# Two edits to a sparse-attention and expert layer: the compressed branch multiplied with the exponentials stationary, and 24 instead of 64 sums of ranks

## The chip, the cores and the metric

The kernel runs on one core of a Trainium2 chip. The metric is the device time of one execution in microseconds (us). Five engines work side by side, each through its own queue in order: TensorE (PE in the profile, its weight loads PEld), VectorE (DVE), ScalarE (ACT), GpSimd (POOL) and SyncE (SP), which here issues the DMAs.

## The reference

The input is x of 8 sequences, 512 tokens, 256 channels. It is normalised, and two branches are added to it.

```python
xn = _layernorm(x)
x + _L0_attn_ref(xn, ...) + _L0_ffn_ref(xn, ...)
```

Attention has 16 heads of 16 channels. Keys and values are compressed in blocks of 16 tokens (32 blocks). Every token attends in three ways, and gates add the three outputs:

```python
s_b = einsum('bhtd,bhnd->bhtn', q, k_c) / scale
logits_c = where(c_ok, s_b, NEG)                    # 32 compressed blocks
out_c = einsum('bhtn,bhnd->bhtd', softmax(logits_c), v_c)
_, top_idx = top_k(logits_c, 4)                     # four blocks chosen: out_s over their tokens
out = gates[..., 0:1]*merge(out_c) + gates[..., 1:2]*merge(out_s) + gates[..., 2:3]*merge(out_l)
return out @ Wo
```

The second branch is a gated layer of 1024 hidden units plus a product-key expert layer: four heads, each with two sets of 64 keys. The eight best of each set give 64 sums, and the eight best of these choose the experts.

```python
sc, ix = top_k(sim, 8)                              # sx, sy: eight each, in falling order
all_sc = (sx[..., :, None] + sy[..., None, :]).reshape(b, t, H, 64)
scores, pk = top_k(all_sc, 8)
w = silu(einsum('btd,bthkd->bthk', hidden_states, de)) * softmax(scores)
experts_states = einsum('bthk,bthkd->btd', w, ue)
```

## The kernel before

Each sequence (a "row") is cut into four tiles of 128 tokens, so there are 32 tiles t, with t.i = 0 to 3 the place in the row. All stages are Python generators, one job each, that go through the rows, the tiles or the halves of a row (two tiles): layernorm, prepare_keys, prepare_values, queries, logits, select, compressed, weights, products, finish(0), finish(1), choose_experts, route, experts, hidden, project and some small ones.

The order of the instructions is planned when the program is built, by the class Conductor. A job yields the engine that it wants next and the buffers or events that it needs; the Conductor starts the job that can begin first, and among those within 0.12 us of it the one of lowest rank (the tile number plus a constant of the stage; compressed has +0.3). What each instruction will take is booked from a small table: a matmul of fp32 as 1.68 ns for each moving column divided by the number of strips that run side by side (con.share), a DVE instruction as 0.07 us and 1.04 ns an element, and so on. It also books that DVE and POOL instructions with two SBUF inputs keep each other waiting. The engines then run in the order that came out, whatever the real times are.

Buffers come from a Stock: taking one waits until it is free in the plan. The names that matter here:

- banks: four single PSUM banks of 512 fp32 columns; pairs: two double ones for logits and weights. All other PSUM work shares the four. products holds two of them as accumulators until finish has copied them.
- acss: two SBUF buffers for copies of PSUM, used by compressed and by both finish jobs.
- atcs, attnTs: two each. atc is the compressed branch's output by token; attnT is the transposed sum of the three branches, freed when project has multiplied it with Wo.
- vc17s: per row, the compressed values of all heads, 17 columns a head (16 and a one for the sum), block-diagonal over four heads: partitions are 4 heads by 32 blocks.

The compressed branch of a tile (compressed, line 827): exponentials of the 16 x 32 logits on ACT, four transposes into a bank, copy to ecT (4 heads x 32 blocks on the partitions, 128 tokens in the columns, four groups g). Then 16 products, of 32 columns of vc17 as the stationary operand with the 128 tokens of ecT moving, four at a time in the four column strips of the array; the result has channels on the partitions. ACT copies it to an acs; the branch then waits for an atc and an attnT; by_token (line 809) transposes the copy back in four pieces, and DVE divides by the sum and multiplies with the gate. by_token serves the two finish jobs as well. The heads in atc stand in the order j, g (head 4g + j); finish adds its half of them on POOL.

In choose_experts (line 974) DVE finds the eight best and their places of eight sets (top, ixu), makes two comparison tables (big, at_x), then the 64 sums (sums, 8 x 8 for each of four heads), and for each head MAX8 (best) and MATCH_REPLACE8, which marks the eight best in pick. A threshold turns the marks into 0 and 1; the sum over j counts for each i how many partners are chosen (cnt). at_x is multiplied with it, et becomes the exponentials of the ranks, and later sums is filled with their products, multiplied with pick and summed to row. route then builds the 1024 gate weights with DVE and three POOL multiplications or additions of 1024 elements for each of four heads (big, gw).

All engine calls go through one helper at line 160, so the profile shows L160 for every instruction; they are told apart by the names of their tiles (cst holds the identity: psum<-cst,acs is the transposition of an acs).

Of the kernel before, what the change touches and what calls it, by code (L numbers as in the profile page):

```python
# [12 lines left out]
ALU = mybir.AluOpType  # L13
# [3 lines left out]
P = 128  # L17
# [13 lines left out]
NX = NEXP // NK  # L31
EPS = 1e-5
D1 = D + 1

OUT = -1.0e30
BIG = 3.0e38
# [218 lines left out]
def tile_kernel(ctx, tc, x, wq, wk, wqT, wv, wo, wck, wcv, wga, bga, wgu, bg, bu, wd, bd,  # L255
# [98 lines left out]


    v17s, vl17s = stock("v17_", 2, [P, NT, H * D1 + D]), stock("vl17_", 2, [P, NT - 1, 8 * D1 + D])
    vc17s = stock("vc17_", 2, [P, H * D1 + D])
    for st_, fill in ((v17s, 1.0), (vl17s, 0.0), (vc17s, 0.0)):
        for it in st_.items:
            pool.memset(it[0], fill)  # L360
# [40 lines left out]
    top, ixu = buf("top", [P, 2 * PH, KPH]), buf("ixu", [P, 2 * PH, KPH], U32)  # L401
    ix = buf("ix", [P, KPH, 2 * PH], BF16)
    at_x = buf("at_x", [P, KPH, NX, PH], BF16)
    sums, pick = buf("sums", [P, PH, KPH, KPH]), buf("pick", [P, PH, KPH, KPH])
    best, row = buf("best", [P, PH, KPH]), buf("row", [P, PH, KPH])
    cnt, et = buf("cnt", [P, KPH, PH], BF16), buf("et", [P, 2 * PH, KPH])
    past, rz = buf("past", [P, PH, KPH]), buf("rz", [P, PH])
# [401 lines left out]
    def by_token(acs, dst, gates):  # L809

        pt = yield PE, banks
        p4 = pt.ap.rearrange("p (a g d) -> p a g d", a=4, g=4)
        for a in range(4):
            pe.transpose(p4[:, a].rearrange("p g d -> p (g d)"), acs.ap[:, a, :], ident)
        acs.free()
        rzn = yield DVE, rzs
        po = p4.rearrange("p a g d -> p (a g) d")
        vec.reciprocal(rzn.ap, po[:, :, D])
        n = gates.shape[1]
        for b in range(n):  # L820
            c = slice(16 // n * b, 16 // n * (b + 1))
            vec.scalar_tensor_tensor(dst[:, c], po[:, c, :D], gates[:, b:b + 1],
                                     bc(rzn.ap[:, c], 2, D), ALU.mult, ALU.mult)
        pt.free()
        rzn.free()

    def compressed(t):

        s, i = t.row, t.i
        yield ACT, t.ev("ec")  # L830
        act.activation(t.ec.ap, t.ec.ap, AF.Exp)
        pt, ecT = yield PE, banks, ecTs
        for g in range(4):
            pe.transpose(heads4(pt.ap)[:, g, :],
                         t.ec.ap[:, 4 * g:4 * g + 4, :].rearrange("p h n -> p (h n)"), ident)
        t.ec.free()
        yield ACT,
        act.copy(ecT.ap, heads4(pt.ap))
        pt.free()
        yield None, s.ev("vc"), s.ev("gates")  # L840

        pt, acs = yield PE, banks, acss
        con.share = 4
        for j in range(4):
            for g in range(4):
                c = D1 * (4 * g + j)
                mm(heads4(pt.ap)[32 * g:32 * g + 32, j, :], s.vc17.ap[:, c:c + 32], ecT.ap[:, g, :],
                   start=j == 0, stop=j == 3, skip_group_check=True, tile_position=(0, 32 * g))
        con.share = 1
        ecT.free()  # L850
        t.done("pc")
        yield ACT,
        act.copy(acs.ap, heads4(pt.ap))
        pt.free()
        t.atc, t.attnT = yield None, atcs, attnTs
        yield from by_token(acs, t.atc.ap, s.gt.ap[:, 2, i:i + 1])
        t.done("atc")

    def weights(t):
# [85 lines left out]
    def finish(jp):  # L945
        def body(t):
            s, i = t.row, t.i
            yield None, t.ev("pv"), t.ev("atc")
            acs, at2h = yield ACT, acss, at2s
            act.copy(acs.ap, heads4(t.acc[jp].ap))  # L950
            t.acc[jp].free()
            at2 = at2h.ap
            yield from by_token(acs, at2.rearrange("p b j (g d) -> p (b j g) d", d=D),
                                s.gt.ap[:, 0:2, i])
            t.done(f"at{jp}")
            at = at2[:, 0].rearrange("p j d -> p (j d)")
            yield POOL,
            pool.tensor_tensor(at, at, at2[:, 1].rearrange("p j d -> p (j d)"), ALU.add)
            pool.tensor_tensor(at, at, t.atc.ap[:, 8 * jp:8 * jp + 8, :].rearrange("p h d -> p (h d)"),
                               ALU.add)  # L960
            t.done(f"sum{jp}")
            pt = yield PE, banks
            pe.transpose(pt.ap[:, :P], at, ident)
            at2h.free()
            yield ACT,
            act.copy(t.attnT.ap[:, jp, :], pt.ap[:, :P])
            pt.free()
            t.done(f"attn{jp}")
            if jp == 1:
                yield None, t.ev("sum0")  # L970
                t.atc.free()
        return body

    def choose_experts(t):

        i = t.i
        yield None, t.row.ev("xn")
        pt = yield PE, banks
        for kc in range(2):
            mm(pt.ap, t.row.xnT.ap[:, kc, i * P:(i + 1) * P], wf_s[:, kc, :], start=kc == 0,  # L980
               stop=kc == 1)
        sim = pt.ap.rearrange("p (h k) -> p h k", k=NK)
        for h in range(2 * PH):
            if h % 2 == 0:
                yield DVE,
            vec.max(out=top[:, h, :], in_=sim[:, h, :])
            vec.max_index(out=ixu[:, h, :], in_max=top[:, h, :], in_values=sim[:, h, :])

        t.ed = yield DVE, eds
        ed = t.ed.ap  # L990
        vec.tensor_tensor(ed[:, :, :NK], sim[:, PH:, :], bc(top[:, PH:, 0], 2, NK), ALU.subtract)
        vec.tensor_tensor(ed[:, :, NK:], sim[:, :PH, :NX], bc(top[:, :PH, 0], 2, NX), ALU.subtract)
        pt.free()
        vec.tensor_copy(ix.rearrange("p j h -> p h j"), ixu)

        ayh = yield DVE, bigs
        at_y = ayh.ap.bitcast(BF16).rearrange("p (j y h) -> p j y h", y=NK, j=KPH)
        vec.tensor_tensor(at_y, bc(ytab, 1, KPH), bc(ix[:, :, PH:], 2, NK), ALU.is_equal)
        yield DVE,
        vec.tensor_tensor(at_x, bc(ytab[:, :NX], 1, KPH), bc(ix[:, :, :PH], 2, NX), ALU.is_equal)  # L1000

        vec.tensor_tensor(sums, bc(top[:, :PH, :], 3, KPH), bc(top[:, PH:, :], 2, KPH), ALU.add)
        for h in range(PH):
            if h % 2 == 0:
                yield DVE,
            flat = sums[:, h].rearrange("p i j -> p (i j)")
            vec.max(out=best[:, h, :], in_=flat)
            vec.match_replace(out=pick[:, h].rearrange("p i j -> p (i j)"),
                              in_to_replace=best[:, h, :], in_values=flat, imm_value=BIG)
        yield DVE,  # L1010
        vec.tensor_scalar(pick, pick, HALF_BIG, None, ALU.is_gt)
        with nc.allow_low_precision(reason="counts up to 8"):
            vec.tensor_reduce(cnt.rearrange("p j h -> p h j"), pick, AX.X, ALU.add)


        vec.tensor_tensor(at_x, at_x, bc(cnt, 2, NX), ALU.mult)
        vec.tensor_tensor(et, top, bc(top[:, :, 0], 2, KPH), ALU.subtract)
        yield ACT,
        act.activation(et, et, AF.Exp)
        act.activation(ed, ed, AF.Exp)  # L1020
        pt, t.rc = yield PE, banks, rcs
        pr = pt.ap[:, :PH * (NK + NX)]
        for j in range(KPH):
            rank = bconst("ranks")[:, j * P:(j + 1) * P]
            mm(pr[:, :PH * NK], rank, at_y[:, j].rearrange("p y h -> p (y h)"),
               start=j == 0, stop=False, skip_group_check=True)
        for j in range(KPH):
            mm(pr[:, PH * NK:], identb, at_x[:, j].rearrange("p x h -> p (x h)"),
               start=False, stop=j == KPH - 1, skip_group_check=True)
        ayh.free()  # L1030
        yield ACT,
        for lo, n in ((0, NK), (PH * NK, NX)):
            act.copy(t.rc.ap[:, lo:lo + PH * n].rearrange("p (h y) -> p h y", y=n),
                     pr[:, lo:lo + PH * n].rearrange("p (y h) -> p h y", y=n))
        pt.free()
        yield DVE,
        vec.tensor_tensor(sums, bc(et[:, :PH, :], 3, KPH), bc(et[:, PH:, :], 2, KPH), ALU.mult)
        vec.tensor_tensor(pick, pick, sums, ALU.mult)
        yield DVE,
        vec.tensor_reduce(row, pick, AX.X, ALU.add)  # L1040
        vec.tensor_reduce(rz, row, AX.X, ALU.add)
        vec.reciprocal(rz, rz)
        vec.tensor_tensor(ed[:, :, NK:], ed[:, :, NK:], bc(rz, 2, NX), ALU.mult)

        t.last = yield DVE, lasts
        vec.scalar_tensor_tensor(past, ix[:, :, :PH].rearrange("p j h -> p h j"), float(NX), row, ALU.is_ge, ALU.mult)
        vec.tensor_tensor(past, past, bc(rz, 2, KPH), ALU.mult)
        vec.tensor_reduce(t.last.ap, past, AX.XY, ALU.add)
        t.done("r")
# [199 lines left out]
```

## Time and profile before

| | |
|---|---|
| median of 4 runs | 1877.21 us (1869.95 to 1881.16) |
| profiled execution, its own time | 1877.63 us |
| its span, first to last instruction | 1875.8 us |
| granted TensorE clock | 0.966 |
| PSUM to acs copies on ACT | 96, 55.6 us busy |
| transposes of acs on PE | 384, 55.7 us busy |
| products of ecT with vc17 on PE | 1024 instructions, 34.5 us busy |
| DVE on sums, both uses | 64, 41.7 us busy |
| MAX8 and MATCH_REPLACE8 of the sums | 128 each, 28.1 and 26.7 us busy |

Busy time is the union of the instructions' spans. Matmuls overlap, so that of PE is not the sum of what each costs; the distance from one start to the next in the timeline is nearer to it. A row of the profile reads: line, engine, operation, tiles (output, then inputs), shape, count, then busy us, mean ns of one, and the idle time in front with what ended it. In the timeline a row has the start, the duration, the engine, the operation and the number of instructions merged in it.

### The profile page before, as it was taken

To read this page: it belongs to the slowest core of one execution; us is meant where nothing else is said; L and a number is where in the kernel's file an instruction comes from. 1 tells how busy PE (TensorE), PEld (TensorE's weight loads), DVE (VectorE), ACT (ScalarE), POOL (GpSimd) and SP (SyncE) were. 2 spreads that over 40 slices of the span, in tenths; PEclk is the share of its full clock that TensorE was granted. 3 is DMA by queue.
4 is the path that set the end of the run, shared out by engine and by line. 5 is a ranking of instruction groups with operands and counts; after the bars stand their busy time and mean duration, and the time that the engine had idled before them with its cause. 6 is when DMAs were issued, how large, how long until landed. Compare 5 with 4: busy or idle time off the path is not lost.

```text
span 1875.8 us, 47619 instructions
## 1 busy us (share of the span) xinstructions
PE 1704.3 (91%) x19208; PEld 1277.4 (68%) x19208; DVE 1476.5 (79%) x5292; ACT 692.6 (37%) x1370; POOL 1022.6 (55%) x789
## 2 busy tenths in 40 slices
PE   4899989999989988899899998989989899998989
PEld 2677756777767766677577766767767677676657
DVE  2588897978879789768879868778787877969982
ACT  1343423434245232443334433344333333343133
POOL 2066637545666356655356552756546556474663
PEclk9899989999999999999899999999999999998999
DMA  5010100111000100010000110001000010100000
GB/s 174 10 39 28 31 18 8 35 41 32 24 24 25 36 19 30 24 42 25 15 28 29 36 31 19 18 25 41 25 24 24 19 36 25 30 19 18 29 24 18
DMA packets 55068, 56.11 MB, mean 30 GB/s; under 512 B 21696, under 2 KB 38080, under 8 KB 54848
## 3 DMA queue, kind: packets, MB, share of 16 engines
q1 hardware_dynamic: 54848, 53.07, 9.6%
q8 instruction: 151, 2.47, 0.5%
q14 instruction: 69, 0.57, 0.1%
HBM read 48.02 MB, written 4.19 MB: 28 GB/s over the span
## 4 chain that ended last, share of the span: by engine, by line
PE 62%; DVE 30%; issue 3%; ACT 2%; POOL 1%; SPq 1%; DMA 1%; DVEq 0%; ACTq 0%
PE psum L160 62%; DVE bm L160 4%; DVE big L160 3%; DVE ixu L160 2%; DVE mr L160 2%; DVE pick L160 2%; DVE ml L160 1%; DVE aT L160 1%; DVE at_x L160 1%; DVE sums L160 1%; ACT wT L160 1%; DVE top L160 1%; DVE junk L160 1%; DVE hT L160 1%; DVE xg L160 1%
## 5 line engine op out<-in xcount | busy, mean ns | idle before, releaser
L160 POOL TENSOR_TENSOR big<-big,ed 128x1024 f32<-128x1024 f32 x224 | 488.6, 2181 | 427.8 <-DVE big L160 388.1
L160 ACT ACTIVATE wT<-psum 128x1024 f32<-128x1024 f32 x224 | 219.3, 1023 | 169.5 <-PE psum L160 169.3
L160 PE MATMUL psum<-xnT,wb 128*128 128x256 f32 x1024 | 255.7, 394 | 22.5 <-DVE aT L160 13.7
L160 DVE TENSOR_REDUCE bm<-psum 128x32 f32<-128x512 f32 (+2 forms) x224 | 200.2, 911 | 74.8 <-PE psum L160 74.6
L160 PEld LDWEIGHTS psum<-xnT,wb 128*128 128x128 f32 x1024 | 193.0, 196 | 59.5 <-DVE aT L160 14.5
L160 POOL TENSOR_TENSOR gw<-gw,big 128x1024 f32<-128x1024 f32 x96 | 229.6, 2392 | 6.7
L160 PE MATMUL psum<-k,q 32*128 32x384 f32 (+3 forms) x1024 | 186.6, 469 | 1.6 <-DVE ml L160 1.6
L160 DVE SCALAR_TENSOR_TENSOR big<-rc 128x1024 f32<-128x1024 f32 x128 | 166.2, 1299 | 6.3 <-POOL gw L160 4.0
L160 PE MATMUL psum<-qx,k 32*128 32x128 f32 (+1 forms) x4352 | 154.7, 273 | 11.8 <-DVE ml L160 9.8
L160 PEld LDWEIGHTS psum<-qx,k 32*128 32x128 f32 (+1 forms) x4352 | 128.0, 177 | 49.1 <-issue 30.2
L160 PE MATMUL psum<-wT,v 128*32 128x128 f32 x3584 | 138.2, 279 | 16.1 <-ACT wT L160 15.3
L160 PEld LDWEIGHTS psum<-wT,v 128*32 128x32 f32 x3584 | 87.0, 109 | 80.1 <-ACT wT L160 37.0
L160 PE MATMUL psum<-xnT,deT_s 128*128 128x128 f32 x1024 | 133.2, 285 | 4.1 <-DVE yo L160 1.7
L160 PEld LDWEIGHTS psum<-xnT,deT_s 128*128 128x128 f32 x1024 | 126.3, 200 | 14.1 <-DVE yo L160 1.8
L160 PE MATMUL psum<-wd_s,hT 128*128 128x256 f32 x512 | 125.1, 390 | 3.5 <-DVE hT L160 2.9
L160 DVE SCALAR_TENSOR_TENSOR aT<-aT,psum 128x512 f32<-128x512 f32 x128 | 87.1, 680 | 48.2 <-ACT aT L160 32.7
L160 ACT ACTIVATE xg<-psum,bgh 128x256 f32<-128x256 f32 x128 | 61.0, 477 | 165.1 <-PE psum L160 163.3
L160 PE MATMUL psum<-ue_s,aT 128*128 128x256 f32 x512 | 119.5, 384 | 1.8 <-DVE aT L160 1.8
L160 PEld LDWEIGHTS psum<-wd_s,hT 128*128 128x128 f32 x512 | 95.5, 194 | 21.3 <-DVE hT L160 3.8
L160 PEld LDWEIGHTS psum<-ue_s,aT 128*128 128x128 f32 x512 | 94.6, 190 | 18.4 <-DVE aT L160 2.0
L160 PEld LDWEIGHTS psum<-k,q 32*128 32x128 f32 x1024 | 77.1, 187 | 42.9 <-issue 32.6
L160 DVE SCALAR_TENSOR_TENSOR xg<-psum,xg 128x256 f32<-128x256 f32 x128 | 53.5, 418 | 63.0 <-ACT psum L160 62.8
(161 smaller groups left out, 3193.4 us busy)
## 6 DMA issues: line engine op xcount, KB each, us to landing
wb<-in_wgu SPq DMA_DIRECT2D x128, 256.0 KB, 2.6
xl<-in_x SPq DMA_DIRECT2D x8, 512.0 KB, 4.0
yo<-in_x SPq DMA_DIRECT2D x32, 128.0 KB, 2.1
out<-yo SPq DMA_DIRECT2D x32, 128.0 KB, 1.7
vl<-v SPq DMA_DIRECT2D x96, 8.5 KB, 1.8
deT_s<-in_deT SPq DMA_DIRECT2D x1, 1024.0 KB, 5.2
wd_s<-in_wd SPq DMA_DIRECT2D x1, 1024.0 KB, 7.4
ue_s<-in_ue SPq DMA_DIRECT2D x1, 1024.0 KB, 9.9
```

Of the source, the lines that this page charges most:

```text
L160: return f(*a, **k)
```

## The change

The compressed branch takes each of the four groups of ecT as the stationary operand (128 columns, the tokens) and the 68 columns of vc17 of the four heads of this group as the moving one. The result lies by token at once, heads in order 0 to 15, in one bank. The copy to acs, the transposes and by_token fall away here; DVE divides and scales straight from this bank, and the bank is kept while the branch waits for an atc and an attnT. by_token is left to finish, which now picks its heads from atc through a strided view.

Of the 64 sums of two ranks i and j, only those with (i + 1)(j + 1) at most 8, or a few more, can be among the eight best. Three rectangles hold 24 of them: i = 0 with j = 0 to 7, i = 1 to 3 with j = 0 to 3, i = 4 to 7 with j = 0. sums and pick shrink to 24 columns a head; each filling of sums, the counting into cnt and the summing into row become three instructions, one for a rectangle (for the last, of width 1, a copy in place of a reduction).

```diff
+STEPS = [(0, 1, 8, 0), (1, 3, 4, 8), (4, 4, 1, 20)]
+NS = 24
...
-    vc17s = stock("vc17_", 2, [P, H * D1 + D])
+    vc17s = stock("vc17_", 2, [P, H * D1])
...
-    sums, pick = buf("sums", [P, PH, KPH, KPH]), buf("pick", [P, PH, KPH, KPH])
+    sums, pick = buf("sums", [P, PH, NS]), buf("pick", [P, PH, NS])
...
@@ compressed
-        pt, acs = yield PE, banks, acss
-        con.share = 4
-        for j in range(4):
-            for g in range(4):
-                c = D1 * (4 * g + j)
-                mm(heads4(pt.ap)[32 * g:32 * g + 32, j, :], s.vc17.ap[:, c:c + 32], ecT.ap[:, g, :],
-                   start=j == 0, stop=j == 3, skip_group_check=True, tile_position=(0, 32 * g))
-        con.share = 1
+        pt = yield PE, banks
+        w = 4 * D1
+        for g in range(4):
+            mm(pt.ap[:, g * w:g * w + w], ecT.ap[:, g, :], s.vc17.ap[:, g * w:g * w + w],
+               start=g == 0, stop=g == 3, skip_group_check=True)
         ecT.free()
         t.done("pc")
-        yield ACT,
-        act.copy(acs.ap, heads4(pt.ap))
+        t.atc, t.attnT = yield None, atcs, attnTs
+        rzn = yield DVE, rzs
+        po = by_head(pt.ap[:, :H * D1])
+        vec.reciprocal(rzn.ap, po[:, :, D])
+        vec.scalar_tensor_tensor(t.atc.ap, po[:, :, :D], s.gt.ap[:, 2, i:i + 1], bc(rzn.ap, 2, D),
+                                 ALU.mult, ALU.mult)
         pt.free()
-        t.atc, t.attnT = yield None, atcs, attnTs
-        yield from by_token(acs, t.atc.ap, s.gt.ap[:, 2, i:i + 1])
+        rzn.free()
         t.done("atc")
@@ finish
-            pool.tensor_tensor(at, at, t.atc.ap[:, 8 * jp:8 * jp + 8, :].rearrange("p h d -> p (h d)"),
-                               ALU.add)
+            atj = at.rearrange("p (j g d) -> p j g d", j=2, g=4)
+            pool.tensor_tensor(atj, atj, t.atc.ap.rearrange(
+                "p (g j) d -> p j g d", j=4)[:, 2 * jp:2 * jp + 2], ALU.add)
@@ choose_experts
-        vec.tensor_tensor(sums, bc(top[:, :PH, :], 3, KPH), bc(top[:, PH:, :], 2, KPH), ALU.add)
+        def steps(table):
+            return [table[:, :, o:o + n * w].rearrange("p h (i j) -> p h i j", j=w)
+                    for _, n, w, o in STEPS]
+        def pairs_of(tab):
+            return [(bc(tab[:, :PH, f:f + n], 3, w), bc(tab[:, PH:, :w], 2, n))
+                    for f, n, w, _ in STEPS]
+        for dst, (a, b) in zip(steps(sums), pairs_of(top)):
+            vec.tensor_tensor(dst, a, b, ALU.add)
         for h in range(PH):
...
+            vec.max(out=best[:, h, :], in_=sums[:, h, :])
+            vec.match_replace(out=pick[:, h, :], in_to_replace=best[:, h, :], in_values=sums[:, h, :],
+                              imm_value=BIG)
...
-            vec.tensor_reduce(cnt.rearrange("p j h -> p h j"), pick, AX.X, ALU.add)
+            for (f, n, w, _), p_ in zip(STEPS, steps(pick)):
+                dst = cnt[:, f:f + n, :].rearrange("p j h -> p h j")
+                if w > 1:
+                    vec.tensor_reduce(dst, p_, AX.X, ALU.add)
+                else:
+                    vec.tensor_copy(dst, p_[:, :, :, 0])
...
-        vec.tensor_tensor(sums, bc(et[:, :PH, :], 3, KPH), bc(et[:, PH:, :], 2, KPH), ALU.mult)
+        for dst, (a, b) in zip(steps(sums), pairs_of(et)):
+            vec.tensor_tensor(dst, a, b, ALU.mult)
         vec.tensor_tensor(pick, pick, sums, ALU.mult)
...
-        vec.tensor_reduce(row, pick, AX.X, ALU.add)
+        for (f, n, w, _), p_ in zip(STEPS, steps(pick)):
+            if w > 1:
+                vec.tensor_reduce(row[:, :, f:f + n], p_, AX.X, ALU.add)
+            else:
+                vec.tensor_copy(row[:, :, f:f + n], p_[:, :, :, 0])
```

More of the change, by code (lines that the diff above doesn't have):

```diff
@@ L818, in by_token @@
         vec.reciprocal(rzn.ap, po[:, :, D])
-        n = gates.shape[1]
-        for b in range(n):
-            c = slice(16 // n * b, 16 // n * (b + 1))
+        for b in range(2):
+            c = slice(8 * b, 8 * b + 8)
             vec.scalar_tensor_tensor(dst[:, c], po[:, c, :D], gates[:, b:b + 1],
@@ L1005, in choose_experts @@
                 yield DVE,
[L1006 to L1009, printed above, removed]
+            vec.max(out=best[:, h, :], in_=sums[:, h, :])
+            vec.match_replace(out=pick[:, h, :], in_to_replace=best[:, h, :], in_values=sums[:, h, :],
+                              imm_value=BIG)
         yield DVE,
```

## The prediction

> **What bounds the kernel.** I read the page first, then the chain, then the groups of the two places that are edited, then the timeline around them. The page:
>
> ```profile
> span 1875.8 us, 47619 instructions
> PE 1704.3 (91%) x19208; PEld 1277.4 (68%) x19208; DVE 1476.5 (79%) x5292; ACT 692.6 (37%) x1370; POOL 1022.6 (55%) x789
> PE 62%; DVE 30%; issue 3%; ACT 2%; POOL 1%; SPq 1%; DMA 1%; DVEq 0%; ACTq 0%
> ```
>
> TensorE is the bound and VectorE the second: the chain that ended last lies 62% on one and 30% on the other, and ScalarE and GpSimd hardly appear. So 62% of 1875.8 = 1163 us of PE's 1704 busy us are on the path, 0.68 of it. The chain's own list by line gives DVE pick 1.8% and DVE sums 1.2%, together 56 us; the groups that write these two tiles (11.8 + 26.7 + 12.2 + 21.2 and 26.3 + 15.4) are busy 114 us. So half of this VectorE work is on the path. I use 0.68 and 0.5 as prices of a microsecond of PE and of DVE.
>
> The compressed branch, by groups (count, then busy us, mean ns):
>
> ```profile
> L160 PE MATMUL psum<-cst,acs 128*128 128x128 f32 x384 | 55.7, 280 | 3.7 <-ACT acs L160 3.1 <-DVE atc L160 0.3
> L160 PE MATMUL psum<-ecT,vc 128*32 128x128 f32 x1024 | 34.5, 275 | 2.4 <-ACT ecT L160 2.0 <-ACT qx L160 0.4
> L160 DVE TENSOR_TENSOR sums<-top 128x256 f32<-128x256 f32 x32 | 26.3, 821 | 0.0
> L160 DVE TENSOR_TENSOR et<-top 128x64 f32<-128x64 f32 x32 | 10.8, 337 | 0.0
> ```
>
> An fp32 product is two instructions, a transpose one: 32 a tile for the 16 products, 4 for the transposes (384 over 32 tiles and three uses).
>
> **TensorE.** What one costs is read from distances in the timeline, not from its 0.27 us:
>
> ```profile
> 911.82 0.33 PE L160 MATMUL psum<-cst,at 128*128 128x128 f32 x1 [0.68 <-POOL at L160]
> 912.07 1.08 PE L160 MATMUL psum<-ecT,vc 128*32 128x128 f32 x32
> 913.09 0.33 PE L160 MATMUL psum<-cst,at 128*128 128x128 f32 x1
> ...
> 913.25 1.95 PE L160 MATMUL psum<-xnT,deT_s 128*128 128x128 f32 x16
> ...
> 9.89 1.87 PE L160 MATMUL psum<-wga_s,big 128*128 128x3 f32 x8 [9.89 <-DMA big<-in_wqT]
> ...
> 19.77 2.47 PE L160 MATMUL psum<-hT 128*128 128x128 f32 x10 [0.58 <-DMA hT<-in_keysT]
> ```
>
> Old products: (1.08 - 0.27) / 31 = 0.026 us each, 0.84 a tile, since four column strips run together. New: 4 products, 8 instructions, each with a full 128-column stationary and 68 moving columns. With 128 moving columns one costs (1.95 - 0.28) / 15 = 0.112. Do 68 cost less? The start-up stretch says no: with 3 moving columns the spacing is (1.87 - 0.35) / 7 = 0.22, with 128 it is (2.47 - 0.42) / 9 = 0.23 (PE work runs at half pace there: four transposes take 1.09 at 35.90, later 0.66); loading the stationary sets it. So I take 8 x 0.112 = 0.90, +0.06 a tile, +1.9 us; the other end, pace by columns (0.060 each), would be 0.48, -11.5 us. The code books 4 x 68 columns at 1.68 ns = 0.46 for it, which I do not believe.
> Transposes removed: 4 x 0.11 (eight take 1.04 at 907.83) = 0.44, 14.1 us. Change of array shape: the batch starts 0.25 after the lone transpose and releases the array 0.21 after its own last start, where like follows like in 0.11; two changes of 0.10 go where both neighbours are full-array, none or some are added where a neighbour is tiled. I take one a tile, 3.2 us (0 to 6.4). PE no longer waits for the ScalarE copy: PEld waited 13.2 us for acs in all, a third is 4.4. Sum: -14.1 - 3.2 - 4.4 + 1.9 = -19.8 us of PE; on the path x 0.68 = -13.5.
>
> **ScalarE and GpSimd.** 32 copies of acs at 0.59 go, 19 us of an engine at 37%: hidden by PE, nothing beyond the wait already counted. GpSimd adds atc from a strided view: 64 additions at 0.54; a tenth more is 3 us, hidden (POOL 1% of the chain). The smaller vc17 saves start-up fill only. The DVE division and scaling keep their sizes; since they now wait on a product booked 0.44 us too short, at most 32 x 0.44 = 14 us of DVE waiting, a sixth of it if it hits as rarely as the reciprocals do now (16 waits in 96): about 1 us on the path, left out. Behind a waiting reciprocal on VectorE stand the next evacuations, as now.
>
> **VectorE, work.** Per tile, TENSOR_TENSOR takes 0.42 for 256 and 0.22 for 64 elements, so 0.15 + 1.04 ns each; and a following independent instruction starts 0.08 before the end of the last:
>
> ```profile
> 907.58 0.43 DVE L160 TENSOR_TENSOR at_x<-at_x,cnt 128x512 bf16<-128x512 bf16 x1
> 907.92 0.22 DVE L160 TENSOR_TENSOR et<-top 128x64 f32<-128x64 f32 x1
> 908.06 1.22 DVE L160 TENSOR_REDUCE bm<-psum 128x64 f32<-128x1024 f32 x1
> ```
>
> Each table in three pieces of 32, 48 and 16: 0.185 + 0.20 + 0.17 - 0.16 = 0.39 against 0.42, twice. Each counting or row reduction in three (reductions 0.42 for 256, 0.19 for 32): 0.40 against 0.42, twice. So the splits give 0.10. MAX8 over 24 takes 0.168 (the t<-lg row of that width) against 0.219, four times: 0.20. MATCH_REPLACE8 lies between 0.164 (20 wide) and 0.173 (28) against 0.209, four times: 0.16. pick times sums 0.42 to 0.25: 0.17; threshold 0.29 to 0.21: 0.08. In all 0.71 a tile, 22.7 us.
> [...]
>
> **VectorE, waits for GpSimd.** Two-input instructions stretch when GpSimd works:
>
> ```profile
> 1005.68 1.37 DVE L160 TENSOR_TENSOR at_x<-cbf,ix 128x512 bf16<-128x512 bf16 x1
> 1006.98 2.12 DVE L160 TENSOR_TENSOR sums<-top 128x256 f32<-128x256 f32 x1
> ...
> 1004.33 4.49 POOL L160 TENSOR_TENSOR big<-big,ed 128x1024 f32<-128x1024 f32 x2 [2.71 <-DVE big L160]
> ```
>
> at_x ends when the first POOL product does, sums when the second does: one DVE instruction per POOL instruction, and behind it in VectorE's queue stand the MAX8s and the bm and aT evacuations whose banks PE waits for. The change adds four such instructions and two copies a tile. Each may lose as little as past (mean 0.212 against 0.193 at best, 0.02) or as much as sums<-top (0.82 against 0.42, 0.40). The nearest row is et<-top, small and directly behind another: 0.337 - 0.218 = 0.12. So 6 x 32 x 0.12 = 23 us (4 to 77), which eats the 22.7. I put VectorE at 0 (on the path -9 to +27).
>
> **Banks.** The product's bank is now kept while the branch waits for an attnT; before, an SBUF copy waited. In the seventh tile the batch runs at 391.77, and the attnT it needs comes free at the projection at 404.87; the batches at 613, 1073, 1299 and 1526 wait 14, 3, 17 and 13 us likewise: 60 us with three single banks for four. Against it every tile asks for one bank fewer. PE is busy 28.00 of 28 us in 391 to 419. I take 0; a quarter of PE's pace lost in all 60 us is 15.
>
> **Sum.** The profiled run took 1877.63 us (span 1875.8), 0.4 above the median 1877.21. 1877.6 - 13.5 + 0 + 0 = 1864.1; against the median 1864.
>
> **Rivals.**
> A, the sum: PE falls by 20 us, VectorE stays. 1864, chance 0.45.
> B, slower: the small VectorE instructions meet GpSimd one by one as sums did at 1006.98. At 0.40 each they cost 192 x 0.40 = 77 where the lesser work saves 23: VectorE loses 54, 27 of it on the path, 1877.6 - 13.5 + 27 = 1891. The sign turns where their waits eat both gains: PE's 13.5 and VectorE's 22.7 x 0.5 = 11.4 on the path are 49.8 us of VectorE, over 192 instructions 0.26 each. For it: GpSimd is busy 55%. Against: after at_x, et lost 0.12 only. Chance 0.20.
> C, no change: the bank kept for attnT costs its 15: 1879, or half of that, 1872. Against: one transposing bank less. Chance 0.18.
> D, more: the 68 columns set the pace (another -11.5 - 1.9 = -13, 0.68 of it 9), and small VectorE work is not delayed (-9): 1846. Against: the 3-column row. Chance 0.17.
> The order on every engine is planned anew from the booked costs, so waits move that no row prices; I leave 10 us for that at both ends.
>
> **Numbers.** About 0.5% (9 us) is what a measurement of this kernel can tell from no change. A and D are faster: 0.62; C: 0.18; B: 0.20. The range reaches from D less a part of the re-planning, 1842, to B, 1890.
>
> **What would show it.** Right: no acs use by the branch (64 copies, 256 transposes), ecT as stationary in 256 instructions spaced near 0.11 (0.06 would be D); MAX8 near 0.17; sums pieces whose mean exceeds their best by about 0.12 (0.4 would be B). Wrong: PE waits for atc well above today's 22 us (C), or PE busy falling by 20 us with its idle time growing as much.

## The result: no faster in the order that was drawn

The changed kernel takes 1880.27 us (median of 52 runs) against 1877.96 (78 runs of the kernel before): a ratio of 1.0014 with a 95% interval of 1.0007 to 1.0021. The forecast of 1864 was 16 us too low: the change was to be faster and is not, though 1880 lies inside the range of 1842 to 1890. The page of the changed kernel (span, busy time by engine, share of the chain by engine):

```profile
span 1876.7 us, 46039 instructions
PE 1689.6 (90%) x18312; PEld 1266.1 (67%) x18312; DVE 1486.1 (79%) x5548; ACT 671.1 (36%) x1338; POOL 1012.1 (54%) x789
PE 57%; DVE 34%; issue 3%; ACT 3%; POOL 1%; SPq 1%; DMA 1%; DVEq 0%; ACTq 0%
```

TensorE is busy 14.7 us less (1704.3 before) and the span is 0.9 us longer, so the time in which PE is not busy grew by 15.6 us, from 171.5 to 187.1. VectorE is busy 9.6 us more, though it was given less to do. The groups of the two edited places (count, then busy us, mean ns of one):

```profile
L164 PE MATMUL psum<-vc,ecT 128*128 128x68 f32 x256 | 35.3, 282 | 1.6 <-ACT ecT L164 1.2 <-DVE aT L164 0.4
L164 PE MATMUL psum<-cst,acs 128*128 128x128 f32 x256 | 36.1, 284 | 1.9 <-ACT acs L164 1.7
L164 DVE TENSOR_TENSOR sums<-top 128x32 f32<-128x32 f32 (+2 forms) x96 | 31.9, 385 | 0.0
L164 DVE COPY row<-pick 128x16 f32<-128x16 f32 x32 | 16.4, 511 | 0.0
L164 DVE MAX8 best<-sums 128x8 f32<-128x24 f32 x128 | 22.8, 178 | 0.8
```

The work is what the prediction described: a third of the transposes of acs is gone, 256 products stand in place of 1024, MAX8 takes 0.178 us instead of 0.219. What the products cost is read from the timeline:

```profile
969.11 1.11 PE L164 MATMUL psum<-vc,ecT 128*128 128x68 f32 x8
970.06 0.60 PE L164 MATMUL psum<-cst,gw 128*128 128x128 f32 x4
```

(1.11 - 0.28) / 7 = 0.119 us from one product instruction to the next, and 0.95 from the first to the transposes that follow.

A part of the lost time is seen in PE's waits. PE's waits for atc (in all, times, longest) in the changed kernel, and then the same list before with three neighbours that are used below:

```profile
PE psum L164 <- DVE atc L164: 29.4, 7, 8.0
```

```profile
PE psum L160 <- DVE aT L160: 24.2, 12, 5.9
PE psum L160 <- DVE atc L160: 22.2, 10, 6.2
PE psum L160 <- DVE hT L160: 15.9, 13, 3.0
...
PE psum L160 <- DVE xn L160: 10.1, 7, 6.1
```

Fewer waits for atc, but longer ones. Counting every wait of PE above 2.5 us after the first 40 us of the trace, there are 14 that last 61.0 us together, against 9 with 37.3 us before. One of them, from the timeline of PE in the changed kernel:

```profile
1363.75 0.60 PE L164 MATMUL psum<-cbf 128*128 128x512 bf16 x2
1370.98 2.07 PE L164 MATMUL psum<-kcbd,q 128*128 128x128 f32 x8 [6.62 <-DVE atc L164]
...
1376.20 1.08 PE L164 MATMUL psum<-cst,ext 128*128 128x128 f32 x4 [2.73 <-DVE aT L164]
1377.09 3.66 PE L164 MATMUL psum<-xnT,deT_s 128*128 128x128 f32 x16
```

And the stretches around it (us, then busy time of PE, PEld, DVE, ACT and POOL, then the granted clock, DMA share and GB/s):

```profile
1364.40:1371.00 6.60, 0.02 (x1) 0.03 (x1) 6.43 (x28) 0.00 (x0) 1.53 (x2) 0.77 0.00 0
1371.00:1381.70 10.70, 7.97 (x63) 6.94 (x64) 9.82 (x29) 1.88 (x4) 5.42 (x6) 0.50 0.01 2
1381.70:1395.00 13.30, 12.61 (x170) 9.73 (x169) 12.50 (x25) 5.84 (x12) 7.54 (x3) 1.00 0.15 56
```

PE waits 6.6 us for a bank that VectorE has yet to read; VectorE is busy for 6.43 of these 6.60 us with work that stands before it in its queue. Then the granted clock is 0.50 for 10.7 us: the 16 deT products take 3.66 us, where they took 1.95 in the kernel before, and four transposes 1.08 instead of 0.60. So this long wait is paid a second time, with some 4 us by an estimate (half of the 7.97 busy).

### The profile page after: what moved, and what is told of

Read it like the earlier page. It is cut to its first block, busy times and chain, and to the rows that moved or that the text cites. A ratio compares the mean times of both kernels' runs of the same rounds, so it can differ in the third digit from the quotient of the medians.

```text
span 1876.7 us, 46039 instructions
## 1 busy us (share of the span) xinstructions
PE 1689.6 (90%) x18312; PEld 1266.1 (67%) x18312; DVE 1486.1 (79%) x5548; ACT 671.1 (36%) x1338; POOL 1012.1 (54%) x789
## 4 chain that ended last, share of the span: by engine, by line
PE 57%; DVE 34%; issue 3%; ACT 3%; POOL 1%; SPq 1%; DMA 1%; DVEq 0%; ACTq 0%
PE psum L164 57%; DVE bm L164 5%; DVE big L164 4%; DVE ixu L164 2%; DVE sums L164 2%; DVE hT L164 1%; DVE ml L164 1%; DVE aT L164 1%; DVE pick L164 1%; DVE mr L164 1%; ACT wT L164 1%; DVE at_x L164 1%; DVE xg L164 1%; DVE junk L164 1%; DVE top L164 1%
## 5 line engine op out<-in xcount | busy, mean ns | idle before, releaser
L164 PE MATMUL psum<-xnT,wb 128*128 128x256 f32 x1024 | 255.4, 394 | 18.3 <-DVE hT L164 14.9
L164 DVE SCALAR_TENSOR_TENSOR big<-rc 128x1024 f32<-128x1024 f32 x128 | 160.7, 1255 | 15.8 <-POOL gw L164 13.8
L164 PE MATMUL psum<-wT,v 128*32 128x128 f32 x3584 | 141.8, 284 | 19.7 <-ACT wT L164 18.3
L164 PE MATMUL psum<-cbf 128*128 128x512 bf16 (+2 forms) x344 | 98.3, 370 | 10.0 <-DVE bm L164 9.8
```

Of the source, the lines that this page charges most:

```text
L164: return f(*a, **k)
```

## The experiments

Each expectation says what its theories mean; H, N and P change from one round to the next. P, from e5 on: the terms of the sum are about right, and the order that was planned from the new booked costs is a bad one. Q: orders planned with the 24 sums booked cheaply are bad for the new branch, other orders are alike. N: the edits, or the one in question, give nothing. All runs are compared with the kernel before on the same chip; ratios below are to that kernel.

**e1_branch and e2_sums: one edit each.** Each has its part of the change as shown above and nothing of the other; the order is planned anew for each.

```diff
 e1_branch
+            mm(pt.ap[:, g * w:g * w + w], ecT.ap[:, g, :], s.vc17.ap[:, g * w:g * w + w],
...
 e2_sums
+    sums, pick = buf("sums", [P, PH, NS]), buf("pick", [P, PH, NS])
...
```

> The branch edit alone, all 64 sums kept. Theory W (the gain of PE is there, and VectorE's extra waits for GpSimd in the 24 sums ate it): 1861 to 1868 us, ratio 0.991 to 0.995, PE busy 15 to 20 us less than before. Theory H (the bank that the branch keeps until VectorE and an attnT are there costs what PE gains): ratio 0.998 to 1.004, PE's waits for atc well over the 22 us of before. Theory R (any re-plan moves the time by some us either way): anything within 0.5% of before, with no link to the terms of the sum.

> The 24 sums alone, the old branch kept. Theory W: 1885 to 1892 us, ratio 1.004 to 1.008: VectorE busy 10 to 15 us more than before, in sums, row and cnt. Theory H: 1866 to 1877, the 24 sums gain or do nothing. Theory R: within 0.5% either way.

Measured: e1 1860.83 us, 0.9932 [0.9907, 0.9957]; e2 1865.69, 0.9949 [0.9931, 0.9967]. Each alone is faster, both together are not: in the orders drawn for them the parts do not add up. No theory fits both runs: e1 lies where W had it, e2 19 us below W's least and inside H's range.

**e3_sums_oldplan: the 24 sums in the order of before.** The planner books what the 64 sums took, so every instruction keeps its old place.

```diff
+        con.size = PH * KPH * KPH
         for dst, (a, b) in zip(steps(sums), pairs_of(top)):
             vec.tensor_tensor(dst, a, b, ALU.add)
+            con.mute = True
+        con.size, con.mute = None, False
...
```

> The 24 sums alone, but booked at the cost of the 64, so that the order of every other instruction on every engine is that of before, and only the execution differs. Theory W: slower than before by 3 to 10 us (ratio 1.002 to 1.005), since waits for GpSimd do not depend on the re-plan. Theory H: faster by 5 to 11 us (22.7 us of VectorE work less, half of it on the path). Theory R: this one is faster by 5 to 11 us and the kernel with only the 24 sums and its own plan is not.

Measured: 1865.79 us, 0.9945 [0.9924, 0.9967], that is 10 us less, with no order to thank for it. W is out; R is too, since the same sums in their own order (e2) are just as fast. Its page, and two of its groups:

```profile
span 1864.9 us, 47875 instructions
PE 1697.0 (91%) x19208; PEld 1271.1 (68%) x19208; DVE 1467.7 (79%) x5548; ACT 691.4 (37%) x1370; POOL 1017.6 (55%) x789
```

```profile
L164 DVE TENSOR_TENSOR sums<-top 128x32 f32<-128x32 f32 (+2 forms) x96 | 25.6, 320 | 0.0
L164 DVE COPY row<-pick 128x16 f32<-128x16 f32 x32 | 13.1, 411 | 0.0
```

VectorE is busy 8.8 us less than before, and the span is 10.9 us shorter. PE is busy 7.3 us less although not one of its instructions was touched: a part of PE's 91% is slow or held-up matmuls, not work. The granted clock is 0.50 for 105.8 us of this profile and for 126.3 us of that before, so a part of the 10 us may be clock.

**e4_replan, e6_after_replan, e9_branch_replan: another order, no other work.** The width within which the planner counts starts as equal goes from 0.12 to 0.11 us, in before, in the changed kernel and in e1.

```diff
-    NEAR = 0.12
+    NEAR = 0.11
```

> The kernel before, with the planner's width for near starts 0.11 instead of 0.12 us: the same work in another order. Theory R: 4 to 15 us away from before, either way. Theories W and H: within 3 us of before.

> The whole change, with the planner's width for near starts 0.11 instead of 0.12 us: same work, another order. Theory P: away from the 1880 us of the whole change by 8 us or more, probably below. Theory I: 1876 to 1885.

> The branch edit alone in another order (the planner's width for near starts 0.11 instead of 0.12 us). Theory P (what an order is worth scatters by 10 us or more, whatever was edited): 1850 to 1885 us, and more than 5 us away from the 1861 of the same edit in its first order. Theory Q (an order made with the 24 sums booked cheaply is worse with the new branch, other orders are alike): 1858 to 1864.

Measured: before 1881.0, 1.0027 [1.0012, 1.0042]; changed 1883.38, 1.0041 [1.0026, 1.0056]; branch alone 1901.67, 1.0144 [1.0117, 1.0171]. e4 is 4 to 5 us from before, at the near end of R. e6 moved by 3 us, where P had 8 or more and theory I had this very place; e9 lies 17 us above P's range and far from Q's. The last is the plainest: the pages of e1_branch and of e9_branch_replan, the same instructions in two orders.

```profile
span 1855.9 us, 45750 instructions
PE 1686.6 (91%) x18312; PEld 1265.9 (68%) x18312; DVE 1466.5 (79%) x5292; ACT 674.5 (36%) x1338; POOL 1020.7 (55%) x789
```

```profile
span 1895.4 us, 45785 instructions
PE 1703.1 (90%) x18312; PEld 1276.7 (67%) x18312; DVE 1478.7 (78%) x5292; ACT 673.4 (36%) x1338; POOL 1014.2 (54%) x789
```

39.5 us apart, of which 16.5 is PE busier and 23.0 PE not busy. The long waits are not the difference: above 2.5 us e1 has 11 with 45.6 us and e9 12 with 46.1, so nearly all of the 23.0 is in shorter ones. And the granted clock is 0.50 for 119.6 us in e1 and 150.7 in e9; half of the difference, 15.6 us, is by this estimate about what PE is busier. A single order says nothing about an edit worth 14.

**e5_both_branchplan, e10_both_branchplan_replan, e11_both_branchplan_replan2: both edits, the sums booked as 64.** The order is then that of the branch edit alone: e5 has that of e1, e10 that of e9, e11 that of width 0.13. The diff is that of e3 laid on the changed kernel, e10 and e11 with another NEAR:

```diff
-    NEAR = 0.12
+    NEAR = 0.11   # e10;  0.13 in e11
```

> Both edits, with the 24 sums booked at the cost of the 64, so that the order of every other instruction is that of the branch edit alone (1861 us). Theory P (the two halves add, and the whole loses only because of the order that the planner made for it): 1848 to 1853 us, ratio 0.984 to 0.987 (16 + 11 us less than before). Theory I (the two halves really collide, through the bank that is kept or through waits for GpSimd): 1870 to 1882, ratio 0.996 to 1.003, as the whole change.

> Both edits, the 24 sums booked at the cost of the 64, width 0.11: the order is that of the branch edit alone with width 0.11. Theories P and Q: 4 to 10 us below that kernel, as 1856 stands to 1861 with width 0.12. Q also: 1853 to 1860.

> Both edits, the 24 sums booked at the cost of the 64, width 0.13. Theory P: anywhere from 1848 to 1883. Theory Q: 1853 to 1860.

Measured: e5 1855.9, 0.9888 [0.9862, 0.9914]; e10 1894.62, 1.0084 [1.0062, 1.0107]; e11 1872.61, 0.9978 [0.9959, 0.9998]. e5 is the fastest kernel of this study: the whole change, 21 us below the kernel before, 24 us below the same work in the order that was drawn for it. It lies 3 us above P's range and 14 below that of theory I, so the two edits do not collide in every order. e10 lies 7 us below e9, as P and Q had it, but Q's 1853 to 1860 came in neither e10 nor e11. And the 24 sums gain in a kept order each time: e3 0.55%, e5 against e1 0.44%, e10 against e9 0.60%, e11 against the branch alone at width 0.13 (e14 below) 0.51%, 8 to 11 us. In the pages of these pairs VectorE is busy 8.8, 12.5, 17.1 and 15.0 us less.

**e7_booked and e8_bank_late: two causes by name.** e7 books the four products at 0.86 us instead of 0.46, near the 0.95 of the changed kernel's timeline; e8 takes atc and attnT before the bank, so that the bank isn't kept while the branch waits (rival C).

```diff
 e7_booked
+        con.share = w / P
         for g in range(4):
...
+        con.share = 1
 e8_bank_late
+        t.atc, t.attnT = yield None, atcs, attnTs
         pt = yield PE, banks
...
-        t.atc, t.attnT = yield None, atcs, attnTs
```

> The whole change, with the four products of the branch booked as if 128 columns moved (0.86 us in place of 0.46), which is what the stationary loads make them cost. Theory B (the planner puts VectorE's division and what follows it on PE too early because it books the products at half their time): 1850 to 1862, PE's waits for atc well under the 29 us of the whole change. Theory P without B: anywhere between 1850 and 1885. Theory I: 1876 to 1885.

> The whole change, with atc and attnT taken before the bank of the products, so that the bank is never kept while the branch waits for an attnT. Theory I by the bank: 1850 to 1862, PE's waits for atc under 15 us. Theory P: anywhere between 1850 and 1885, PE's waits for atc not the cause.

Measured: e7 1871.87, 0.9978 [0.9961, 0.9995]; e8 1886.9, 1.006 [1.0041, 1.0078]. PE's waits for atc are 18.2 us in e7 and 20.2 in e8, well under the 29.4 of the changed kernel, and yet e7 is 10 us slower than B had it and e8 25 slower than theory I had it. Both plans differ from that of the changed kernel in more than the point in question, and their steps of -8 and +7 us are within what the order alone does. Neither decides anything by itself; e8 gives C no support.

**e12_after_replan2, e13_before_width13, e14_branch_width13, e15_sums_width11, e16_sums_width13: a table of orders.** They complete four kernels by three widths. The diff is the line of NEAR again, 0.11 in e15, 0.13 in the others:

```diff
-    NEAR = 0.12
+    NEAR = 0.13   # e12, e13, e14, e16;  0.11 in e15
```

> The whole change, the 24 sums booked at their own size, width 0.13. Theory P: anywhere from 1848 to 1885. Theory Q: 1876 to 1886, as with widths 0.12 and 0.11.

> The kernel before, its width of choice 0.13 instead of 0.12; no work changes, only the order. It completes a table of four kernels (before, branch alone, sums alone, both) by three orders (widths 0.11, 0.12, 0.13). Theory P (each edit gains what its instructions say, the order scatters by some 20 us about that): before at 1865 to 1900, and the mean of its three orders above the mean of both edits, 1874.7 (1883, 1880, 1860), by 10 us or more, so this run at 1895 or above if the scatter is even, though three orders leave 12 us of doubt. Theory N (the two edits together give nothing in any order, 1860 was a lucky one): the mean of before within 3 us of 1874.7, so this run near 1866.

> Branch edit alone, width 0.13. So far 1861 and 1902 at 0.12 and 0.11. Theory P: the two are ends of the scatter about the forecast of 1864, this one at 1845 to 1885. Theory N: the branch edit gives nothing, the two are ends of a scatter about 1880, this one at 1870 to 1895.

> 24 sums alone, width 0.11. Under the order of before and its own order at 0.12 it took 1866 both times. Theory P: about 10 us below the same width of before (1881) plus or minus the scatter, 1851 to 1891. Theory N: 1880 plus or minus 20 alike; only the mean of the three widths, 1866 and near it against 1878, tells the two apart.

> 24 sums alone, width 0.13. Theory P: 1850 to 1890, the mean of the three widths about 10 us below the mean of before at the same widths. Theory N: the means within 3 us of each other.

Measured, in us: e12 1860.29, e13 1886.63, e14 1883.57, e15 1878.83, e16 1867.31. As ratios to the kernel before:

| | width 0.11 | 0.12 | 0.13 | mean |
|---|---|---|---|---|
| before | 1.0027 | 1 | 1.0050 | 1.0026 |
| sums alone | 1.0008 | 0.9949 | 0.9945 | 0.9967 |
| branch alone | 1.0144 | 0.9932 | 1.0029 | 1.0035 |
| both | 1.0041 | 1.0014 | 0.9912 | 0.9989 |

e12 lies in P's range and 16 us below Q's, so Q is out. e13 lies 8 us below what P asked for an even scatter and 20 above N; e14 fits both; e15 and e16 fit P. The mean of before is 7 us above that of both edits, between P's 10 and N's 3.

(Each single ratio has an interval of about 0.002 to either side; 0.001 is 1.9 us.) The sums gain in both pairs of rows, 0.0059 alone and 0.0046 on top of the branch, 9 to 11 us. The branch does not: 0.0009 and 0.0022 slower in the mean, from steps between -0.0068 and +0.0117. Three orders can't rule out a gain of some us, but the forecast of 13.5 (0.0072) was not to be seen, although PE is busy 15.5 us less in the branch kernels than in before (means of the three pages: 1693.1 and 1708.6). So P holds for the sums and not for the branch, which the last two runs take up.

**e17_branch_oldplan and e18_branch_oldplan13: the branch edit in the order of before.** The planner books the old products, the copy and the transposes; only the new products are issued, at the place of the transposes and into their bank. No other instruction moves, and the bank is taken after the waits for atc and attnT, as before. e17 has the order of before, e18 that of e13. So these two runs lack what the edit itself may gain by a bank that comes free, and ecT, of which there is one, is held until the later place.

```diff
-                mm(heads4(pt.ap)[32 * g:32 * g + 32, j, :], s.vc17.ap[:, c:c + 32], ecT.ap[:, g, :],
+                con.book("PE", "matmul", (heads4(pt.ap)[32 * g:32 * g + 32, j, :],
...
-        act.copy(acs.ap, heads4(pt.ap))
+        con.book("ACT", "copy", (acs.ap, heads4(pt.ap)), {})
...
+        pt = yield PE, banks
+        for g in range(4):
+            con.book("PE", "transpose", (), {})
+            con.mute = True
+            mm(pt.ap[:, g * w:g * w + w], ecT.ap[:, g, :], s.vc17.ap[:, g * w:g * w + w],
+               start=g == 0, stop=g == 3, skip_group_check=True)
+            con.mute = False
```

> Branch edit alone under the order of before: the planner books the old products, copy and transposes, but only the four new products are issued, at the place of the transposes, into their bank (so the bank is taken after the waits for atc and attnT, as before, and one bank stands unused where the old products were). Every other instruction keeps its place. Theory P (the terms are right, the drawn orders hid them): PE busy 15 to 20 us less, idle time of PE as before (166), so 1864, 1860 to 1868. Theory H (half): the other engines set the pace as often, PE's gain comes back as PE waiting: PE busy 15 less, idle 8 more, 1870. Theory N (PE's work in the branch is worth nothing, it all comes back as waiting): 1877, within 4 us.

> The same under another order of before, that of width 0.13 (1886.6 with the old branch). Theory P: 1873, 1869 to 1877. Theory H: 1880. Theory N: 1887, within 4 us. If the two runs gain differently by more than 8 us, what PE's work is worth depends on the order too, and 0.68 is no constant of the kernel.

Measured: e17 1873.04 beside 1873.2 of the kernel before on that chip, 0.9988 [0.997, 1.0006], so 2 us less, from 6 less to 1 more; e18 1878.12, 1.0024 [1.0004, 1.0044], where e13 had 1.0050 [1.0030, 1.0070], 5 us less with 5 of doubt. The expectations stood on 1877 for the kernel before, which ran at 1873.2 here, so they are read 4 us lower: P's 13 us less and H's 7 lie outside the interval of e17, and N, by which PE's work in the branch is worth nothing, is the nearest. In e18 P's 13 less is outside as well, but H's 7 is inside, and so is a part of N's range. The page of e17_branch_oldplan, and its list of PE's waits:

```profile
span 1875.5 us, 45772 instructions
PE 1696.1 (90%) x18312; PEld 1271.0 (68%) x18312; DVE 1479.1 (79%) x5292; ACT 674.7 (36%) x1338; POOL 1023.8 (55%) x789
```

```profile
PE psum L160 <- DVE aT L160: 26.9, 16, 6.0
PE psum L160 <- DVE atc L160: 21.2, 9, 5.9
PE psum L160 <- DVE hT L160: 17.2, 16, 3.1
...
PE psum L160 <- DVE xn L160: 11.5, 9, 6.0
```

The removed work is real: summed from start to start, without the waits, the products went from 32.3 to 30.2 us and the transposes of acs from 48.0 to 31.2, together 18.9 us. But PE is busy only 8.2 us less and not busy 7.9 us more: the other matmuls, the same ones in the same order, took 10.7 us longer, and the waits for aT, hT and xn each grew by 1.3 to 2.7 us. In this pair of pages PE came earlier to the same waits.

The pages of e13_before_width13 and e18_branch_oldplan13 read otherwise:

```profile
span 1889.4 us, 47643 instructions
PE 1712.1 (91%) x19208; PEld 1281.9 (68%) x19208; DVE 1476.9 (78%) x5292; ACT 690.0 (37%) x1370; POOL 1019.4 (54%) x789
```

```profile
span 1871.1 us, 45796 instructions
PE 1692.8 (90%) x18312; PEld 1269.1 (68%) x18312; DVE 1478.3 (79%) x5292; ACT 671.1 (36%) x1338; POOL 1020.0 (55%) x789
```

Here 20.1 us were freed, PE is busy 19.3 us less and not busy only 1.0 more, and the span is 18.3 us shorter. But the profiled run of e13 is 4.6 us above its median and that of e18 5.2 below, so these two executions say less than the medians, which put the gain at 5 us with 5 of doubt. That PE's gain comes back as waiting is thus seen in one of two orders and in single executions.

Part of it may be clock: the mean granted clock of the runs of e17 is 0.9657, that of the 23 runs of before beside them 0.9693, and 0.0036 of some 1700 busy us is 6 us, an estimate. In the other order it is 0.9598 in e18 and 0.9637 in e13, on two chips.

## Why the prediction was wrong, step by step

**The step that failed first: the price of PE's microseconds.** The prediction multiplied 19.8 us of PE by 0.68, because 62% of the span is PE on the chain. In the kept orders 18.9 and 20.1 us were freed, and 2 and 5 arrived, a price of 0.1 and 0.25. The chain says who ended last, not what would be late next; in e17's page PE waits for VectorE's aT, hT and xn behind these products anyway. That this is the whole cause is not shown, as e18's page has no such growth of PE's idle time.

The terms below the price were fair, with one exception. The transposes gave 16.8 us (14.1 predicted). The products with the change of array shape gave 2.1 (1.3 predicted, 3.2 for the shape less 1.9; a tile's new products take 0.94 us, forecast 0.90, its old ones had taken 1.01 with the shape, forecast 0.94). The exception is the 4.4 us for the copy that PE no longer waits for: the 13.2 us were waits of the weight loads, they are still 12.4 in e17 and 13.4 in the changed kernel, and PE's own waits for acs were 3.1 us before and 2.4 in e17. So the 19.8 came near 18.9 because two errors met.

**VectorE at 0 was wrong too, in the other direction.** The splitting and the waits for GpSimd were of the right kind: in e3 each of the pieces starts about 0.08 us before the end of the one in front (in the changed kernel 0.077 to 0.085, the medians of the four places), as the prediction took from et and at_x. In e3 the pieces of sums<-top take 0.32 us in the mean, where the median of the three sizes is 0.166 to 0.199 (0.14 more, 0.12 forecast), and the work shrinks about as forecast (MAX8 0.178 and MATCH_REPLACE8 0.168 us). They do not cancel fully: VectorE gains 8.8 us of busy time in e3, which lies inside the bounds, and 12.5 to 17.1 in the three other pairs of kept orders, and these bring 10, 8, 11 and 10 us, about 0.7 of a microsecond for each one instead of 0.5. So in these orders a microsecond of VectorE was worth more than one of PE. The two errors nearly cancel: in the order of before the edits give 2 and 10 us, against 13.5 and 0 forecast, so 1865 beside 1864; that nearness is luck. The sum is an estimate; both edits together were not run in the order of before.

**The step that cost the rest: re-planning.** It was said to be left 10 us at both ends, but the range ends 4 us below D and 1 short of B, and the forecast has nothing for it. Same work in other orders spans 1860 to 1883 us for the changed kernel, 1861 to 1902 for the branch alone, 1856 to 1895 for both with the sums booked as 64, 1877 to 1887 for before. From the estimate of 1865 to 1880 are 15 us that the drawn order costs, a size that every table row with the branch edit shows. What they are made of is not shown. The drawn order has five more long PE waits than before, but e6, the same kernel at 1883 us, has 11 with 43.5 us and e12, at 1860, 11 with 45.0. What does go with the time in these three is the half clock: 133.3 us in the changed kernel, 138.0 in e6, 106.2 in e12. It isn't a rule: e5, the fastest, has 140.8.

**The rivals.** A failed as told. B: the small VectorE pieces do meet GpSimd, more so in the drawn order (0.385 and 0.511 us in the groups above, VectorE busy 9.6 us more than before; a mean 0.20 above the median, where B had 0.40), but in kept orders they leave a gain, so they don't turn the sign. C: the time fell into C's place, and PE's waits for atc grew as it said, but its cause is not what decides: in e17 the bank is taken as late as before, PE's waits for atc are 21.2 us, and the gain is missing all the same; in e8, with 20.2, the time is 1887. D is out: 0.119 us from start to start, not 0.06. What the prediction named as the sign of being wrong, PE busy less with its idle time growing as much, is what came: 14.7 less and 15.6 more.

**What stays open.** Why one order has more idle time of PE and more half clock than another was not traced to a rule; nor why the removed PE work arrives in the profiled run of e18 and not in that of e17; nor why the rows with the branch edit scatter more (0.021 and 0.013) than those without (0.005 and 0.006). With three orders each, that may be chance.

## What to carry to other kernels

Before a microsecond off the busiest engine is counted, look for the next wait of that engine behind it: if another engine's queue ends that wait, the gain can turn into waiting, and work cut in that other queue may bring more, as it did here. Where a planner orders the instructions, each edit also draws a new order; measure an edit in the kept order (book the old costs) and the whole change in several orders, and keep the best one. Here that turned the same work from 1880 into 1856 us.

## What the runs showed of the hardware

In these profiles a long wait of TensorE is mostly followed by half clock. Over the profiles of before, after and the 18 experiments, counted from 40 us on, a stretch of granted clock 0.50 begins during the wait or within 3.5 us of its end for 9% of PE's waits of 0.15 to 1 us (222 of 2347), 30% of those from 1 to 2 us, 79% from 2 to 3, 93% from 3 to 4.5, and for all 55 above 4.5 us. Most such stretches last 3.4, 6.8 or 10.2 us: in before and after 41 of the 43 that end inside the span, the two others 13.7. What sets these lengths is not shown, and whether other waits close by have a part in the half clock was not examined.

Which small VectorE instructions meet GpSimd was a surprise as well. In e3 the reductions of pick (0.186 to 0.196 us) took the same nearly every time, and of three pieces of sums<-top mainly the first stretches (0.588 in the mean against a median of 0.185; the two behind it 0.206 and 0.166); of the later filling from et it is the first and the third (0.279 and 0.281 against 0.186 and 0.169). The copies of 16 columns, one input and one output, stretch like additions: the one into row 0.411 in the mean against 0.165 (in the changed kernel 0.511, and the one into cnt 0.298 against 0.177). Of the pieces of sums<-top and the copies into row that took over one and a half times the median, 15 of 17 end within 0.4 us of the end of a GpSimd instruction; in the changed kernel 20 of 20 do, where of all 128 it is 56.

With the clock goes the time of a run: within one kernel's runs (158 runs of the 18 experiments, each kernel's mean taken out) the time falls by 1.3 us for each 0.001 that the mean granted clock is higher, with a correlation of -0.79. How much of that is the clock itself and how much the waits that lower it, these runs don't separate.
